# Perceiver, layer 0: a seven-operation weight decode, heads turned earlier, Newton last on GpSimd, and spare buffers in the opening

## The chip, the core and the metric

The kernel runs on one core of a Trainium2 chip, in float32 for nearly all of its matmuls. The metric is the device time of one launch in microseconds; the time of a version is the median of its runs. Five engines work side by side, each through its own list of instructions in order: TensorE (PE; its weight loads are PEld), VectorE (DVE), ScalarE (ACT), GpSimd (POOL) and SyncE (SP), which in this kernel issues nearly all DMAs.

## The reference

`x` is 64 sequences of 32 rows of 256 numbers, and `ctx` 64 sequences of 257 such rows. Six blocks follow one another, each on the layer norm of `x` and added to it:

```python
x = x + _L0_xattn_ref(_layernorm(x), ctx_1024, ctx_1024, ...)
x = x + _L0_attn_ref(_layernorm(x), ...)
x = x + _L0_ffn_ref(_layernorm(x), L0_ffn_weight, L0_ffn_weight_scale, L0_ffn_bias)
x = x + _L1_xattn_ref(_layernorm(x), ctx_1024, ctx_1024, mask, ...)
x = x + _L1_attn_ref(_layernorm(x), ...)
x = x + _L1_ffn_ref(_layernorm(x), ...)
```

The change lies in layer 0. Its two attentions have 16 heads of 16, are causal over 32 positions (the first attends to the first 32 rows of the context), and turn queries and keys by rotary angles: `x1 * cos - x2 * sin`, `x1 * sin + x2 * cos`. Its feed-forward block rounds its input and its weights to 8-bit floats with 4 exponent and 3 mantissa bits ("coarse" numbers). The weights come to the kernel as bytes:

```python
x_scale = jnp.maximum(amax, 1e-12) / FP8_MAX
qinput = (x / x_scale).astype(FP8)
A = qinput.astype(x.dtype) * x_scale
Bm = weight.astype(x.dtype) * weight_scale
out = jnp.einsum('bsk,nk->bsn', A, Bm) + bias
```

Layer 1 (a cross attention over all 257 rows, a gated mixer, a routed mixture of eight experts) is left as it is.

## The kernel before, in words

`x` stays on the chip in four tiles `xs[g]` of 512 rows, each as four row tiles of 128. Layer 0's two attentions on four such groups give eight groups, n = 0 to 7, and `small_attentions` runs them through one hand-written pipeline. All instructions are kept in the order of the program on each engine, so an instruction that waits holds up all behind it on its engine.

The opening loads the inputs (`first_loads`, a generator that issues a few DMAs at each `next`), normalises group 0 and rotates its keys and queries. After it each group n takes four steps, t = 0 to 3, and a step does a piece for several groups:

- `scores`, `sums`, `turned`, `context`, `by_feature` and `project` belong to the row tiles of groups already prepared. A tile goes through them over five steps (the list `line`): scores with `mx` and `sc` on DVE and `e` on ACT; then its sums; then e turned by PE (`ps_t`, `eT`) and the context `o`; then `by_feature` turns the heads' output on PE (`ps_c`) and ACT writes `cT`; then `project` multiplies `cT` by the output weights (`ps_p`) and DVE adds the result to `x`.
- `rotated` prepares the group n+1: one half of its keys (t = 0, 1) or queries (t = 2, 3). PE computes `ps_qk`, DVE writes `part` (times sine), four DMAs copy `part` into `far` with its 32-row blocks swapped, ACT and POOL make `near` (times cosine). It returns an add, `near + far` on POOL, which goes into the list `adds` and writes `kT` or `qT`.
- `spread_keys` writes `kb`, the blocks of keys, from `kT`: in each of a step's two parts one or two of them on ACT, and one on POOL in the first part.
- `values` (t = 0 and 2) computes `v` and writes it to DRAM; `blocks` (t = 3) reads it back into `vb` with eight DMAs.
- `norm_steps` normalises the group n+2, in pieces called through `prepare`: statistics in t = 0; their aggregate, the first guess `r0` and three Newton steps for the root in t = 1 (twelve operations on 128x4 on POOL; for n = 0 nine on DVE); the rows `y` of two tiles in t = 2 and of two in t = 3. `opened` then turns `y` into `yT`.
- `add_bias` adds the output bias row to `x` on POOL.
- `decode_fp8` makes the coarse weights `w8` from the bytes `raw`, two DVE operations a call, on one half of the weights at a time. `first_sides` works on the feed-forward block of the first row group from n = 6 on, and needs `w8` in n = 7.

The adds of a step run early in the next one if that is a t = 0, and late otherwise:

```python
due, adds = adds, []
if t == 0:
    for add in due:
        add()
    due = []
```

Buffers come in rings: `part` has two (p0, p1), `near` two (n0, n1), `far` three; the scores' bank on PE, `pair_bank`, is one. In the opening, keys and queries of group 0 share the rings.

Of the kernel before, what the change touches and what calls it, by code (L numbers as in the profile page):

```python
# [7 lines left out]
F32 = mybir.dt.float32  # L8
BF16 = mybir.dt.bfloat16
I32 = mybir.dt.int32  # L10
U8 = mybir.dt.uint8
AF = mybir.ActivationFunctionType
ALU = mybir.AluOpType
# [3 lines left out]
P = 128  # L17
D = 256
NB, S, SK = 64, 32, 257
H, DH = 16, 16  # L20
NG, NT = 4, 4
GT = NT * P
# [17 lines left out]
R_XO0, R_AO0, R_FF, R_XO1, R_GO, R_SB2, R_RB = 0, 256, 512, 768, 1024, 1280, 1536  # L40
# [24 lines left out]
def perceiver_kernel(ctx: ExitStack, tc: tile.TileContext, a: dict, out: bass.AP):  # L65
# [54 lines left out]
    def turn(ps, src, eye):  # L120
        return kept(nc.tensor.transpose(ps, src, eye))  # L121

    def norm_steps(g, eng=None, apart=False, ts=range(NT), by_act=False):

        x = xs[g]
        n, t0 = len(ts), ts[0]
        st = small.tile([P, n, 6], F32, tag="st", name="st")
        mv = small.tile([P, n, 2], F32, tag="mv", name="mv")
        for t in range(n):
            vector.bn_stats(st[:, t, :], x[:, t0 + t, :])  # L130
        if apart:
            yield
        for t in range(n):
            vector.bn_aggr(mv[:, t, :], st[:, t, :])

        ve = small.tile([P, n], F32, tag="ve", name="ve")
        vector.tensor_scalar(ve, mv[:, :, 1], EPS, None, ALU.add)
        half = small.tile([P, n], I32, tag="half", name="half")
        vector.tensor_scalar(half, ve.bitcast(I32), 1, None, ALU.logical_shift_right)
        r0 = small.tile([P, n], I32, tag="r0", name="r0")  # L140
        vector.tensor_scalar(r0, half, -1.0, float(0x5F3759DF), ALU.mult, ALU.add)
        r = r0.bitcast(F32)
        for _ in range(3):
            sq = small.tile([P, n], F32, tag="sq", name="sq", bufs=6)
            rn = small.tile([P, n], F32, tag="rn", name="rn", bufs=6)
            if eng is vector:
                vector.tensor_tensor(sq, r, r, ALU.mult)
                vector.scalar_tensor_tensor(sq, sq, -0.5, ve, ALU.mult, ALU.mult)
                vector.scalar_tensor_tensor(rn, sq, 1.5, r, ALU.add, ALU.mult)
            else:  # L150
                gpsimd.tensor_tensor(sq, r, r, ALU.mult)
                gpsimd.tensor_tensor(sq, sq, ve, ALU.mult)
                gpsimd.tensor_scalar(sq, sq, -0.5, 1.5, ALU.mult, ALU.add)
                gpsimd.tensor_tensor(rn, sq, r, ALU.mult)
            r = rn
        if by_act:
            off = small.tile([P, n], F32, tag="off", name="off")
            gpsimd.tensor_scalar(off, mv[:, :, 0], -1.0, 1.0, ALU.mult, ALU.mult)
            gpsimd.tensor_tensor(off, off, r, ALU.mult)
        yield  # L160
        y = ypool.tile([P, n, D], F32, tag="y", name="y")
        for t in range(n):
            if by_act:
                scalar.activation(
                    y[:, t, :],
                    x[:, t0 + t, :],
                    AF.Identity,
                    bias=off[:, t : t + 1],
                    scale=r[:, t : t + 1],
                )  # L170
            else:
                vector.tensor_scalar(
                    y[:, t, :],
                    x[:, t0 + t, :],
                    mv[:, t, 0:1],
                    r[:, t : t + 1],
                    ALU.subtract,
                    ALU.mult,
                )
            if t == 1 and n > 2:  # L180
                yield
        return y
# [46 lines left out]
    def proj(ps, w, rhs):  # L229

        for k in range(2):
            mm(ps, lhsT=w(k), rhs=rhs(k), start=(k == 0), stop=(k == 1))
# [13 lines left out]
    def small_attentions(layers, first_loads, decode, sides, load_layer1, layer1):  # L246
# [51 lines left out]
        def opened(it):  # L298
            yT = transposed(it["y"], pa, yTs([P, 2, GT], "yT"))
            it["yT"] = yT  # L300
            if not it["from_ctx"]:
                it["kvT"] = yT

        def rotated(it, i, c):

            src, cs, sn = (
                (it["kvT"], cos, sin) if i == 1 else (it["yT"], cosq, sinq)
# [5 lines left out]
            w, v0 = it["w"], it["v0"]  # L313
            ps = pa([P, GT], "ps_qk")
            proj(ps, lambda k: w[:, i, k, c * P : (c + 1) * P], lambda k: src[:, k, :])

            def by_place(table):
                return table.rearrange("p (o q) -> p o q", o=1).to_broadcast([P, 16, S])
# [2 lines left out]
                return tile_.rearrange("p (b q) -> p b q", q=S)  # L321

            bias = vec[:, v0 + 2 * i + c : v0 + 2 * i + c + 1]
            part = part_([P, GT], "part")
            vector.scalar_tensor_tensor(
                by_seq(part), by_seq(ps), bias, by_place(sn), ALU.add, ALU.mult
            )
# [2 lines left out]
            for at in range(0, P, S):  # L330
                queue = scalar if (it["n"], i, c) == (0, 0, 1) and at >= 2 * S else sync
                queue.dma_start(out=far[at : at + S, :], in_=part[at ^ S : (at ^ S) + S, :])
            near = near_([P, GT], "near")
            if it["n"] > 0:
                scalar.activation(near, ps, AF.Identity, bias=bias)
                gpsimd.tensor_tensor(by_seq(near), by_seq(near), by_place(cs), ALU.mult)
# [166 lines left out]
        it = group(0, fetch(0))  # L503
        next(loads)
        after = group(1, fetch(1))
        next(loads)
        for half in range(2):
            clear(vbs[0][half], vector)
            clear(vbs[1][half], gpsimd)
# [13 lines left out]
            spread_keys(it, 0, 0, part)  # L523
        adds.append(rotated(it, 0, 0))
        adds.append(rotated(it, 0, 1))
        adds[1]()
        for part in range(2):
            spread_keys(it, 0, 1, part)
# [13 lines left out]
        for n in range(len(order) + 1):  # L542
# [3 lines left out]
                after["kb"] = [None, None]  # L546
            kvT = coming = None
            if n + 2 <= last:
                side = norm_steps(order[n + 2][1], None if n else vector, apart=True)
            else:  # L550
                side = sides

# [7 lines left out]
            for t in range(NT):  # L560
# [3 lines left out]
                if n <= last:  # L564
                    if t < 2:
                        kb_now = (now, 1, t)
                    elif after is not None:
                        kb_now = (after, 0, t - 2)
                due, adds = adds, []
                if t == 0:  # L570
                    for add in due:
                        add()
                    due = []
                if kb_now:
                    spread_keys(*kb_now, 0)
                if line[4]:
# [1 line left out]
                if after is None:  # L578
                    next(layer1, None)
                else:  # L580
                    y = prepare(t % 2 == 1)
                    adds.append(rotated(after, *((1, 0), (1, 1), (0, 0), (0, 1))[t]))
                if line[3]:
                    by_feature(line[3])
                prepare(t % 2 == 0)
                if n + 2 > last:
# [1 line left out]
                    next(side, None)  # L588
                if n > 0:
                    add_bias(n - 1, t)  # L590
                if n > 0 and (t % 2 == 0 or n + 2 > last):
                    next(decode, None)
                for add in due:
                    add()
                if kb_now:
                    spread_keys(*kb_now, 1)
                if after is None:
                    next(layer1, None)
                elif t % 2 == 0:
                    values(after, t // 2)  # L600
                    if (n, t) == (0, 0):
                        opened(after)
                elif t == 3:
                    for half in range(2):
                        blocks(after, half)
                    if n + 2 <= last:
                        coming = group(n + 2, kvT)
                        coming["y"] = y
                        opened(coming)
# [22 lines left out]
    def first_loads():  # L632
        def row_load(at, n=D):
            sync.dma_start(
                out=rows[:, at : at + n], in_=a["rows"][at : at + n].partition_broadcast(P)
            )
# [8 lines left out]
        sync.dma_start(out=xs[1], in_=x_view[1])  # L645
        yield
        sync.dma_start(out=xs[2], in_=x_view[2])
        sync.dma_start(out=w_cur[:, 3], in_=a["w_l0x"][:, 3])
        row_load(R_XO0)
        sync.dma_start(out=xs[3], in_=x_view[3])  # L650
        yield
        sync.dma_start(out=raw, in_=a["w_fp8"])
        for at in (R_AO0, R_FF, R_XO1, R_GO):
            yield
            row_load(at)
        for i in range(0, 4, 2):
# [9 lines left out]

    def decode_fp8():

        scratch = sb.tile([P, 4, D], F32, tag="yT", name="scratch")
        u, neg, e_f, scale = (scratch[:, i, :] for i in range(4))  # L670
        bits = scale.bitcast(I32)
        for c in range(2):
            vector.tensor_copy(u, raw[:, c * D : (c + 1) * D])
            vector.tensor_scalar(neg, u, 128.0, None, ALU.is_ge)
            yield
            vector.scalar_tensor_tensor(u, neg, -128.0, u, ALU.mult, ALU.add)
            vector.tensor_copy(bits, u)
            yield
            vector.tensor_scalar(bits, bits, 3, None, ALU.logical_shift_right)
            vector.tensor_copy(e_f, bits)  # L680
            yield
            vector.scalar_tensor_tensor(u, e_f, -8.0, u, ALU.mult, ALU.add)

            vector.tensor_scalar(bits, e_f, 1.0, 120.0, ALU.max, ALU.add)
            yield
            vector.tensor_scalar(bits, bits, 23, None, ALU.logical_shift_left)

            vector.tensor_scalar(e_f, e_f, 1.0, None, ALU.min)
            yield
            vector.scalar_tensor_tensor(u, u, 0.125, e_f, ALU.mult, ALU.add)  # L690
            vector.tensor_tensor(u, u, scale, ALU.mult)
            yield
            vector.tensor_scalar(neg, neg, -2.0, 1.0, ALU.mult, ALU.add)
            vector.tensor_tensor(w8[:, c, :], u, neg, ALU.mult)
            yield

    def linear(g):

# [1355 lines left out]
```

## The time and the profile before

| | |
|---|---|
| time, median of 3 runs | 929.61 us (929.5 to 930.77) |
| profiled execution, its own time | 928.56 us |
| its span, first to last instruction | 926.8 us |
| mean granted clock of PE over the span | 0.973 |
| busy share: PE, PEld, DVE, ACT, POOL | 92%, 63%, 65%, 46%, 54% |
| DVE's first operation on scores (`mx`) | 31.41 us |
| DVE's last `sc` of layer 0 | 223.37 us |
| 40 to 225 us, busy: PE, DVE, ACT, POOL | 170.7, 159.2, 112.8, 125.6 us |

In a row of the timeline the first number is the start in us from the beginning of the span, the second the duration from the first to the last of the instructions that the row joins (x2, x4); then come engine, line, operation, output<-inputs and shapes. SPq and ACTq rows are issues of DMAs. Brackets give how long the engine had been idle ahead of the row and what ended that; where a wait is for several things, the one named is the one that came last by the profile. L106 and L118 are lines of helpers that issue all operations, so rows are told apart by their tiles. A row `q1 ...` or `far<-part SPq ...` of the page's last part gives size and median time from issue to landing.

### The profile page before, as it was taken

What the parts mean: (1) busy time and instruction counts of PE and PEld (TensorE: products, weight loads), DVE (VectorE), ACT (ScalarE), POOL (GpSimd) and SP (SyncE); (2) the same over time, 40 slices, a digit from 0 to 9 for tenths busy, and PEclk for the clock granted to TensorE, in tenths of its full rate; (3) what the DMA queues carried; (4) which work ended last, traced back from release to release, by engine and by line L of the source; (5) the groups of instructions that cost most, each with busy time, mean ns of one, the idle gap of its engine ahead of it and who ended that gap; (6) DMA issues with size and microseconds to landing.
All of it is one profiled execution on the core that took longest, in us unless ns stands there. A gap on an engine that the chain in (4) does not pass through costs nothing. (4 is left out here: it accounts for less than half of the span.)

```text
span 926.8 us, 22828 instructions
## 1 busy us (share of the span) xinstructions
PE 856.0 (92%) x8699; PEld 588.5 (63%) x8699; DVE 605.3 (65%) x1755; ACT 424.1 (46%) x1099; POOL 501.1 (54%) x982
## 2 busy tenths in 40 slices
PE   6899999979899999999999999999889889999993
PEld 3566666656456666666656666565656648888882
DVE  7888888897677677675777666878654872111116
ACT  2566666645555555554555456564443212222210
POOL 3567667764674656564664747656531214555430
PEclk9999999989999999999999999999799979999997
DMA  7445333543110111111110112000001046777758
GB/s 240 140 133 141 85 88 101 132 115 104 53 52 8 46 53 53 52 54 52 53 52 3 52 52 98 2 2 24 2 23 35 24 143 189 235 240 229 216 182 272
DMA packets 66926, 88.79 MB, mean 96 GB/s; under 512 B 32480, under 2 KB 50688, under 8 KB 64768
## 3 DMA queue, kind: packets, MB, share of 16 engines
q1 hardware_dynamic: 63264, 77.75, 27.6%
q0 software_dynamic: 3456, 9.44, 3.1%
q8 instruction: 69, 1.13, 0.5%
q14 instruction: 41, 0.34, 0.1%
q10 hardware_dynamic: 96, 0.13, 0.1%
HBM read 65.80 MB, written 13.11 MB: 85 GB/s over the span
## 5 line engine op out<-in xcount | busy, mean ns | idle before, releaser
L106 ACT ACTIVATE e<-e,xnm 128x257 f32<-128x257 f32 x256 | 127.2, 498 | 51.5 <-DVE xnm L106 45.5
L106 DVE CUSTOM_DVE_ANT_0 e<-ps_s,mask 128x257 f32<-128x257 f32 x256 | 93.5, 421 | 49.6 <-PE ps_s L118 47.9
L118 PE MATMUL ps_k<-ct,w_w_l1x 128*128 128x512 f32 x256 | 122.3, 600 | 1.6 <-ACT yT L106 0.6
L106 POOL TENSOR_SCALAR e<-e,xsm 128x256 f32<-128x256 f32 x256 | 121.8, 496 | 0.0
L118 PE MATMUL ps_v<-w_w_l1x,ct 128*128 128x256 f32 x512 | 121.8, 381 | 0.0
L121 PE MATMUL ps_t<-cst,e 128*128 128x128 f32 x640 | 102.9, 284 | 7.8 <-DVE eT L106 6.9
L106 DVE COPY eT<-ps_t 128x512 f32<-128x512 f32 x128 | 88.0, 687 | 30.3 <-PE ps_t L121 30.1
L118 PEld LDWEIGHTS ps_v<-w_w_l1x,ct 128*128 128x128 f32 x512 | 93.9, 191 | 11.0 <-issue 0.2
L106 POOL TENSOR_TENSOR x<-x,rows 128x256 f32<-128x256 f32 x96 | 71.3, 759 | 46.2 <-ACT y L106 19.4
L106 ACT ACTIVATE kT<-ps_k,vec 128x512 f32<-128x512 f32 x64 | 44.1, 689 | 100.5 <-PE ps_k L118 100.3
L121 PEld LDWEIGHTS ps_t<-cst,e 128*128 128x128 f32 x640 | 72.1, 142 | 26.4 <-DVE eT L106 7.8
L106 ACT ACTIVATE hTr<-ps_h,w 128x256 f32<-128x256 f32 (+1 forms) x80 | 31.4, 450 | 115.0 <-issue 82.7
L106 DVE TENSOR_TENSOR og<-ps_o,b 128x512 f32<-128x512 f32 (+1 forms) x20 | 12.8, 638 | 105.6 <-PE ps_o L118 105.6
L118 PEld LDWEIGHTS ps_k<-ct,w_w_l1x 128*128 128x128 f32 x256 | 44.5, 190 | 41.3 <-issue 35.3
L1817 POOL DMA_INDIRECT r_rows<-og,lv x36 | 35.6, 989 | 60.9 <-DVE og L106 56.0
L118 PE MATMUL ps_h<-ygT,w 128*128 128x256 f32 (+1 forms) x320 | 65.8, 359 | 0.6 <-issue 0.6
L118 PE MATMUL ps_o<-w,hTr 128*128 128x256 f32 x288 | 65.3, 379 | 0.0
L106 ACT COPY v<-ps_v 128x512 f32<-128x512 f32 x80 | 46.4, 582 | 39.5 <-PE ps_v L118 39.4
L106 POOL TENSOR_TENSOR last<-e,xsm 128x4 f32<-128x4 f32 x64 | 13.0, 204 | 88.4 <-DVE xsm L106 88.0
L118 PEld LDWEIGHTS ps_h<-ygT,w 128*128 128x128 f32 x320 | 54.9, 190 | 6.6 <-issue 0.8
L118 PEld LDWEIGHTS ps_o<-w,hTr 128*128 128x128 f32 x288 | 54.4, 190 | 7.2
L106 ACT ACTIVATE kb<-kT,cst 128x256 f32<-128x256 f32 x96 | 45.4, 512 | 26.7 <-POOL kT L106 25.1
(210 smaller groups left out, 1677.2 us busy)
## 6 DMA issues: line engine op xcount, KB each, us to landing
ct<-in_ctxT SPq DMA_DIRECT2D x16, 1024.0 KB, 5.4
w<-in_ew SPq DMA_DIRECT2D x20, 514.0 KB, 3.6
w<-in_ew SPq DMA_DIRECT2D x20, 512.0 KB, 3.7
far<-part SPq DMA_DIRECT2D x126, 64.0 KB, 2.3
v_rows<-v SPq DMA_DIRECT2D x16, 256.0 KB, 2.3
vb<-v_rows SPq DMA_DIRECT2D x64, 64.0 KB, 2.1
r<-r_rows SPq DMA_DIRECT2D x8, 512.0 KB, 8.2
b<-in_eb SPq DMA_DIRECT2D x20, 128.0 KB, 3.8
```

The source lines that it names most:

```text
L106: ins = getattr(self.engine, name)(*args, **kw)
L118: return kept(nc.tensor.matmul(ps, **args))
L121: return kept(nc.tensor.transpose(ps, src, eye))
L1817: wrote = nc.gpsimd.indirect_dma_start(out=r_rows, out_offset=bass.IndirectOffsetOnAxis(ap=write_i[:, at : at + 1], axis=0), in_=o[:, i, : ...
```

## The change

- `decode_fp8`: the byte is shifted so that its exponent and mantissa stand in a float's places, 120 is added to the exponent, small numbers are mended by `u + min(u - 2^-6, 0)`, and the sign is put on. Seven operations on all 512 columns replace 13 on 256 for each half, one a call instead of two, and it is called in even steps alone.
- The adds of a step all run at the head of the next step.
- `rotated` takes the tile whose heads are due and calls `by_feature` right behind its own matmuls, so `ps_c` and `cT` come ahead of `part` and `near` in the order.
- `norm_steps` has one more pause, between `r0` and Newton; Newton is called late in t = 1, behind the key blocks' second part.
- In the opening the keys of group 0 get `part` and `near` in buffers that the scores use later (sc0, sc1, e0, e1). The third set of loads is issued behind the first queries, and the loads are cut into other sets, so that the output weights, the first bias row and `x` of groups 2 and 3 come later, and the bytes `raw` at the end of step t = 3 of n = 0 instead of t = 1.
- `opened` of group 1 moves from step t = 0 of n = 0 to t = 1.

```diff
-    def norm_steps(g, eng=None, apart=False, ts=range(NT), by_act=False):
+    def norm_steps(g, eng=None, apart=False, ts=range(NT), by_act=False, split=False):
...
         r = r0.bitcast(F32)
+        if split:
+            yield
         for _ in range(3):
...
-        def rotated(it, i, c):
+        def rotated(it, i, c, between=None):
...
             proj(ps, lambda k: w[:, i, k, c * P : (c + 1) * P], lambda k: src[:, k, :])
+            if between:
+                by_feature(between)
+            spare = (it["n"], i) == (0, 1)
...
-            part = part_([P, GT], "part")
+            part = sb.tile([P, GT], F32, tag=f"sc{c}", name="part") if spare else part_([P, GT], "part")
...
-            near = near_([P, GT], "near")
+            near = sb.tile([P, GT], F32, tag=f"e{c}", name="near") if spare else near_([P, GT], "near")
...
         after = group(1, fetch(1))
-        next(loads)
...
         adds.append(rotated(it, 0, 1))
+        next(loads)
         adds[1]()
...
-                side = norm_steps(order[n + 2][1], None if n else vector, apart=True)
+                side = norm_steps(order[n + 2][1], None if n else vector, apart=True, split=True)
...
-                due, adds = adds, []
-                if t == 0:
-                    for add in due:
-                        add()
-                    due = []
+                for add in adds:
+                    add()
+                adds = []
...
-                    adds.append(rotated(after, *((1, 0), (1, 1), (0, 0), (0, 1))[t]))
-                if line[3]:
+                    adds.append(rotated(after, *((1, 0), (1, 1), (0, 0), (0, 1))[t], line[3]))
+                if line[3] and after is None:
                     by_feature(line[3])
...
-                if n > 0 and (t % 2 == 0 or n + 2 > last):
+                if n > 0 and t % 2 == 0:
                     next(decode, None)
-                for add in due:
-                    add()
                 if kb_now:
                     spread_keys(*kb_now, 1)
+                prepare(t == 1)
                 if after is None:
                     next(layer1, None)
                 elif t % 2 == 0:
                     values(after, t // 2)
-                    if (n, t) == (0, 0):
-                        opened(after)
+                elif (n, t) == (0, 1):
+                    opened(after)
...
         sync.dma_start(out=xs[2], in_=x_view[2])
+        yield
         sync.dma_start(out=w_cur[:, 3], in_=a["w_l0x"][:, 3])
         row_load(R_XO0)
+        yield
         sync.dma_start(out=xs[3], in_=x_view[3])
         yield
         sync.dma_start(out=raw, in_=a["w_fp8"])
-        for at in (R_AO0, R_FF, R_XO1, R_GO):
+        row_load(R_AO0)
+        for at in (R_FF, R_XO1, R_GO):
             yield
             row_load(at)
...
-        scratch = sb.tile([P, 4, D], F32, tag="yT", name="scratch")
...
+        scratch = sb.tile([P, 2, 2 * D], F32, tag="yT", name="scratch")
+        u, v = (scratch[:, i, :] for i in range(2))
+        bits = u.bitcast(I32)
+        vector.tensor_copy(bits, raw)
+        yield
+        vector.tensor_scalar(
+            bits, bits, 127, 20, ALU.bitwise_and, ALU.logical_shift_left
+        )
+        yield
+        vector.tensor_scalar(bits, bits, float(120 << 23), None, ALU.add)
+        yield
+        vector.tensor_scalar(v, u, -(2.0**-6), 0.0, ALU.add, ALU.min)
+        yield
+        vector.tensor_tensor(u, u, v, ALU.add)
+        yield
+        vector.tensor_scalar(v, raw, 128.0, -2.0, ALU.is_ge, ALU.mult)
+        yield
+        vector.scalar_tensor_tensor(
+            w8.rearrange("p c d -> p (c d)"), v, 1.0, u, ALU.add, ALU.mult
+        )
+        yield
```

More of the change, by code (lines that the diff above doesn't have):

```diff
@@ L667, in decode_fp8 @@
     def decode_fp8():
-        scratch = sb.tile([P, 4, D], F32, tag="yT", name="scratch")
[L670 to L695, printed above, removed]
+        scratch = sb.tile([P, 2, 2 * D], F32, tag="yT", name="scratch")
[19 more added lines that the diff above has]
+        yield
     def linear(g):
```

## The prediction, on record before the result

> **What bounds the kernel now.** I read the page's busy shares first: PE 92%, DVE 65%. The chain that ended last begins at 761 us and says nothing about layer 0, so for the stretch the change touches I went to the timeline, engine by engine, and then to the table of stages.
>
> A group of layer 0 takes four steps, t = 0 to 3; I call that a round and mark its end by T, the start of `part` in step t = 3. From the `part` rows T is 43.78, 67.91, 92.40, 117.26, 142.22 and 167.18 for groups 0 to 5, then 194.55. First the timeline's rows of one round (start, duration, instruction; in brackets the idle time ahead and who ended it):
>
> ```profile
> 93.22 2.74 SPq L106 DMA_DIRECT2D far<-part  x4
> 96.06 4.01 SPq L106 DMA_DIRECT2D vb<-v_rows  x8
> 100.18 3.05 SPq L106 DMA_DIRECT2D far<-part  x4
> 98.28 0.76 DVE L106 SCALAR_TENSOR_TENSOR part<-ps_qk,vec,cst 128x512 f32<-128x512 f32 x1 [1.12 <-PE ps_qk L118]
> 100.26 1.84 DVE L106 TENSOR_SCALAR scratch<-scratch 128x256 int32<-128x256 int32 x2
> 105.90 0.20 POOL L106 TENSOR_TENSOR sq<-r 128x4 f32<-128x4 f32 x1 [3.45 <-DVE r L106]
> 107.97 1.13 PE L118 MATMUL ps_p<-w_w_l0x,cT 128*128 128x256 f32 x4 [1.26 <-ACT cT L106]
> 109.15 1.27 POOL L106 TENSOR_TENSOR near<-near,cst 128x512 f32<-128x512 f32 x1
> 110.37 0.73 POOL L106 TENSOR_TENSOR x<-x,rows 128x256 f32<-128x256 f32 x1
> 111.05 1.27 POOL L106 TENSOR_TENSOR kT<-near,far 128x512 f32<-128x512 f32 x1
> 111.53 1.28 DVE L106 TENSOR_SCALAR y<-x,mv,rn 128x256 f32<-128x256 f32 x2
> 113.72 0.68 DVE L106 TENSOR_REDUCE mx<-pair_bank 128x16 f32<-128x512 f32 x1
> 117.26 0.74 DVE L106 SCALAR_TENSOR_TENSOR part<-ps_qk,vec,cst 128x512 f32<-128x512 f32 x1
> ```
>
> PE pauses about 1.7 us a round (1.26 here for cT, 0.5 for yT in t = 0), so of 24.9 us some 23.2 are PE's own. DVE is full from one `part` to the next except for some 3.5 us of short waits. The ceiling on steady rounds is therefore 1.7 us each, whatever is taken off DVE. SP matters too: eight vb issues stand between the far copies of t = 3 and those of t = 0.
>
> Next, the opening, the place where the weight bytes arrive, and the end of the layer:
>
> ```profile
> 18.08 0.75 DVE L106 SCALAR_TENSOR_TENSOR part<-ps_qk,vec,cst 128x512 f32<-128x512 f32 x1 [2.25 <-DMA far<-part]
> 31.41 0.69 DVE L106 TENSOR_REDUCE mx<-pair_bank 128x16 f32<-128x512 f32 x1 [1.13 <-PE pair_bank L118]
> 47.05 5.10 SPq L106 DMA_DIRECT2D vb<-v_rows  x8
> 52.19 0.45 SPq L106 DMA_DIRECT2D rows<-in_rows  x1
> 50.92 1.10 DVE L106 CAST scratch<-raw 128x256 f32<-128x256 uint8 x1
> 199.55 1.36 DVE L106 TENSOR_TENSOR w<-scratch 128x256 bf16<-128x256 f32 x1
> 202.63 0.69 PE L121 MATMUL ps_c<-cst,o 128*128 128x128 f32 x2 [3.50 <-DVE o L106]
> far<-part SPq DMA_DIRECT2D x126, 64.0 KB, 2.3
> ```
>
> DVE has no wait of any size from 173.06 to about 210, and PE idles for it (1.37, 0.92, 1.14, 3.50 us): here DVE is the bound.
>
> **The decode.** The 26 old operations on 128x256 take 19.4 us in all (timeline rows of scratch): 0.29 us where nothing disturbs, 1.1 where a GpSimd operation is under way. Seven on 128x512 replace them, one in each even step, finished by group 4. The nearest rows of that width are 0.55 (int32 tensor_scalar, at 195.21) to 0.69 (tensor_tensor); I take 0.75 with disturbance, between 0.4 and 1.6. In groups 1 to 5 the saving falls on DVE time in front of PE-bound waits. In groups 6 and 7 it is on the path: from the first decode row of a step to its mx it is 0.55 + 1.47 + 1.20 + 2.13 = 5.35 us. **Tail: -5.4** (between -2, if PE's order takes over, and -7, PE's idle there).
>
> TensorE is granted 0.50 in 204 to 208, after that 3.5 us gap. [...]
>
> **The opening.** The keys' part and near get buffers of their own, so the 2.25 us wait at 18.08 goes, and 1.4 MB (x2, x3, one weight matrix, one row) leave the queue ahead of the far copies. What is late next: kT's add waits for its far copies (18.03 now, perhaps 16.5), then the queries' far copies (four issues of 0.65 us a piece on SP), q's adds at about 24.7 instead of 26.0; the transposes of group 1 no longer stand ahead of the first scores. DVE then has its normalisation and bn_stats of x2, which is now issued on SP behind 14 far copies, near 22, and lands some 4 to 6 us later (x: 6.2 median in the first 60 us). I put the first mx at 27.9 instead of 31.41. From mx to T0 DVE is full (12.4 us) and keeps that length. **Opening: -3.5** (0 to -5).
>
> **The steady round.** cT ahead of near takes cT off the wait for `part`; it ends PE's 1.26 us wait if nothing else is late. But the adds now stand at the head of each step, and GpSimd executes in order. In t = 1 the kT add needs the far copies of t = 0, which SP issues only after the eight vb. Counted from T: far 0.8 to 3.6, vb to 7.7, far again to 10.8, the last issue at 10.1; landing 2.3 later (the page's median): 12.4. Then GpSimd does add 1.27, the keys' block 0.55, near 1.22, row bias 0.7 and, last, Newton: 3.3 from 105.90 to 109.2. Sum 7.0 with gaps: r is ready at T + 19.4. `y` in t = 2 needs r; now y starts at T + 19.1, because Newton came ahead of near, bias and add. Then y 1.28, decode 0.75 and 3.54 from mx to the next `part` (113.72 to 117.26). So T' = T + 25.0 with a decode operation and 24.2 without, against 24.9 now. PE's wait for cT turns into DVE's wait for Newton. Behind y wait mx, sc, o and `part` on DVE; PE waits for o.
>
> Round by round, with the issue times of its own rows: group 2 has a slower vb (5.46) and a row load behind it, far lands at 13.4: 25.9 against 24.49, +1.4. Group 3 has one row load in front: 25.3 against 24.86, +0.5. Group 4 decodes nothing in t = 2: 24.2 against 24.96, -0.8. Group 5 (far rows end later, 13.4): 25.2 against 24.96, +0.2.
>
> Group 1 is worse, because the byte load moves from t = 1 to t = 3 of group 0, where it is issued behind the vb copies: T0 + 8.4, landed 10.75 with the 2.3 us of other 64 KB transfers. The first decode operation, which DVE reaches at T0 + 7.1 (50.92 less 43.78), waits 3.6 us, and mx, o and `part` of t = 1 wait behind it. `part` at 15.3, near on ACT to 16.9, near on GpSimd, bias, Newton to 22.15, then 1.28 + 0.75 + 3.54: 27.7 against 24.13, +3.6. **Rounds: +4.9.** Bounds: -4 if far lands so early that PE sets every round, +8 if y also waits out the next add.
>
> [...] Row: y's first operation took 0.95 and its second 0.33 while the kT add had 0.79 us to run, so y waited for the end of an add; I keep 1.28 for the pair. [...]
>
> **Sum.** -3.5 + 4.9 - 5.4 = -4.0 us, of the profiled execution's 928.56 (span 926.8): 924.56. The median of three runs is 929.61, 1.05 above it, so I forecast 925.6.
>
> **Rivals.** (1) *Far lands in time and PE sets the rounds*: each of groups 2 to 5 saves 1.5 us, group 1 loses 2: -3.5 - 4 - 5.4, 916.7. For it: cT's wait is plain in every round. Against: SP's issue rows are full from T to T + 10.8. Chance 0.12. (2) *Slower: GpSimd's add in t = 1*, held by SP's order, delays Newton and with it y by more than I count. It decides once far lands later than T + 14 or y waits out the add; then rounds cost +9, the opening gives only 2 because x2 comes late, and the tail 4: 932.6. For it: vb took 5.1 to 5.5 us in groups 0 and 1, and loads move behind it. Against: 4.0 later. Chance 0.25. (3) *No change*: gains and losses cancel, the decode's cycles being free where PE or SP sets the pace; 929.6. Chance 0.20.
>
> My forecast, faster by 2 to 7 us, gets 0.43. A measurement of this kernel can tell about 0.2% (1.86 us) from no change. Faster: 0.43 + 0.12 = 0.55, same 0.20, slower 0.25. Range 918 to 932, which leaves out most of rival 1 and the end of rival 2; the forecast's own is 922.5 to 927.7.
>
> **What would show it.** Right: first mx near 28; T0 near 40; a DVE wait of 3 to 4 us for raw at T0 + 7; GpSimd idle ahead of kT's add in t = 1 until some 12.4 us after T, and a DVE wait for rn ahead of y in t = 2; PE without its 1.26 us wait for cT; rounds of 25 us; DVE in groups 6 and 7 some 5 us shorter. Wrong: rounds near 23.3 (no such chain), no wait for raw (the byte load landed sooner), or PE idle past 200 as long as before.

## The result and the profile after

The changed kernel takes 939.42 us, median of 6 runs (934.88 to 943.35), against 929.77 for the kernel before on the same chip: a ratio of 1.0099, 95% interval 1.0077 to 1.0121. The forecast was 925.6 us with a range of 918 to 932; it is slower by 9.7 us instead. The profiled execution is the longest of the six, 943.35 us with a span of 941.6 us. The six spans run from 933.1 us at a mean granted clock of 0.973 to 941.6 us at 0.963: on the whole the longer runs have the lower clock. All that is read from the trace below belongs to this longest execution; it lies 14.8 us above the profiled execution of before (928.56 us), where the medians differ by 9.7.

From the page of the kernel after, the busy shares (engine, busy us, share of the span, instructions): they are within a point of those of before, and tell nothing of the loss.

```profile
PE 864.7 (92%) x8699; PEld 595.1 (63%) x8699; DVE 602.4 (64%) x1734; ACT 425.9 (45%) x1099; POOL 497.6 (53%) x982
```

The timeline of the kernel after, round of group 3 (T = 100.15 to 128.69), rows of SP, DVE, POOL and PE; these stand against the first rows of the prediction:

```profile
103.48 4.00 SPq L106 DMA_DIRECT2D vb<-v_rows  x8
108.08 2.42 SPq L106 DMA_DIRECT2D far<-part  x4
106.75 0.75 DVE L106 SCALAR_TENSOR_TENSOR part<-ps_qk,vec,cst 128x512 f32<-128x512 f32 x1 [1.29 <-PE ps_qk L118]
107.53 0.45 SPq L106 DMA_DIRECT2D rows<-in_rows  x1
108.73 1.49 DVE L106 TENSOR_TENSOR scratch<-scratch 128x512 f32<-128x512 f32 x1
113.19 1.28 POOL L106 TENSOR_TENSOR kT<-near,far 128x512 f32<-128x512 f32 x1 [2.38 <-DMA far<-part]
113.36 1.14 DVE L106 TENSOR_SCALAR ve<-mv 128x4 f32<-128x4 f32 x1
115.19 0.75 DVE L106 SCALAR_TENSOR_TENSOR part<-ps_qk,vec,cst 128x512 f32<-128x512 f32 x1
116.82 1.28 POOL L106 TENSOR_TENSOR near<-near,cst 128x512 f32<-128x512 f32 x1 [1.90 <-ACT near L106]
118.74 0.22 POOL L106 TENSOR_TENSOR sq<-r 128x4 f32<-128x4 f32 x1
121.84 0.20 POOL L106 TENSOR_TENSOR rn<-sq,rn 128x4 f32<-128x4 f32 x1
122.02 1.26 POOL L106 TENSOR_TENSOR kT<-near,far 128x512 f32<-128x512 f32 x1
122.07 1.85 DVE L106 TENSOR_SCALAR y<-x,mv,rn 128x256 f32<-128x256 f32 x2 [2.67 <-POOL rn L106]
123.84 1.48 DVE L106 TENSOR_SCALAR scratch<-raw 128x512 f32<-128x512 uint8 x1
127.03 0.44 PE L121 MATMUL ps_c<-cst,o 128*128 128x128 f32 x2 [2.78 <-DVE o L106]
128.69 0.75 DVE L106 SCALAR_TENSOR_TENSOR part<-ps_qk,vec,cst 128x512 f32<-128x512 f32 x1
```

The chain is the forecast one: SP's vb issues, then far, GpSimd idle 2.38 us ahead of kT's add, near, Newton (twelve operations, 118.74 to 122.04), then y, on which DVE waited 2.67 us, and behind it o, for which PE waited 2.78 us. In the kernel before, the last rn stands at 109.2, T + 16.8; here at T + 21.9. Far lands later, near waits, and y and the decode operation take longer than forecast; only the way from mx to the next `part`, 3.45 us for 3.54, does not. A round of 28.54 us has come of one of 24.86. Far was held here by SP's list and by a late `part` nearly alike: the `part` of t = 0 ends at 107.50, and SP is done with vb and the row load behind it at 107.98. No run moved the vb issues, so SP's share is read from these rows and not tested.

The waits of the kernel after from 40 to 235 us (us in total, times, longest):

```profile
POOL kT L106 <- DMA far<-part: 18.2, 5, 5.4
PE ps_c L121 <- DVE o L106: 16.2, 8, 3.9
DVE y L106 <- POOL rn L106: 13.9, 5, 3.6
DVE scratch L106 <- DMA raw<-in_w_fp: 4.1, 1, 4.1
```

The same waits of the kernel before; no row there has y waiting for rn:

```profile
PE ps_p L118 <- ACT cT L106: 8.0, 7, 1.4
PE ps_c L121 <- DVE o L106: 5.8, 3, 3.5
```

The wait for cT is gone and a larger one has come.

The table of stages of the kernel after, cut at the steps of the granted clock to within 0.05 us (stretch, length, then busy us and instructions of PE, PEld, DVE, ACT, POOL; PEclk; DMA share; GB/s):

```profile
96.89:100.30 3.41, 1.11 (x8) 0.79 (x8) 3.34 (x9) 2.03 (x5) 2.15 (x3) 0.99 0.38 111
100.30:103.71 3.41, 3.41 (x78) 2.49 (x78) 1.75 (x3) 2.44 (x5) 1.95 (x2) 0.51 0.22 56
...
124.19:127.60 3.41, 0.63 (x6) 0.57 (x6) 3.34 (x5) 0.92 (x2) 3.39 (x4) 0.99 0.00 0
127.60:131.01 3.41, 2.92 (x55) 1.72 (x57) 1.83 (x5) 2.59 (x8) 0.71 (x1) 0.50 0.09 23
```

The two stretches in which PE works for 1.11 and 0.63 of 3.41 us are followed by one and by two at half clock: the half clock stands right behind PE's pause for o. Up to 239 us the kernel after has 30.7 us at half clock in six places, three of 3.41 us and three of 6.8 (from 127.6, 182.3 and 216.4 us); before has 10.2 us (from 30.8 and 201.5).

The opening, the arrival of the bytes and the end of the layer, timeline of the kernel after:

```profile
16.55 0.75 DVE L106 SCALAR_TENSOR_TENSOR part<-ps_qk,vec,cst 128x512 f32<-128x512 f32 x1 [0.31 <-PE ps_qk L118]
28.91 0.67 DVE L106 TENSOR_REDUCE mx<-pair_bank 128x16 f32<-128x512 f32 x1
34.60 3.02 PE L118 MATMUL ps_qk<-yT,w_w_l0x 128*128 128x512 f32 x4 [2.88 <-ACT yT L106]
47.18 5.89 SPq L106 DMA_DIRECT2D vb<-v_rows  x8
55.30 0.43 DVE L106 CAST scratch<-raw 128x512 int32<-128x512 uint8 x1 [4.09 <-DMA raw<-in_w_fp]
197.78 3.54 DVE L106 TENSOR_SCALAR y<-x,mv,rn 128x256 f32<-128x256 f32 x4
203.03 0.44 PE L121 MATMUL ps_c<-cst,o 128*128 128x128 f32 x2 [1.30 <-DVE o L106]
217.47 0.69 PE L121 MATMUL ps_c<-cst,o 128*128 128x128 f32 x2 [3.92 <-DVE o L106]
```

The part of 18.08 has lost its 2.25 us and the first mx comes 2.50 us sooner, but T0 is 43.91 (before 43.78), because PE stands 2.88 us for group 1's yT. The bytes cost 4.09 us, for 3.6 forecast. At the end of the layer neither PE's waits nor the half clock have gone: the last sc is at 238.21, 14.84 us later than before.

Split at the T's, those 14.84 us are: opening +0.13 (forecast -3.5), group 1 +5.59 (29.72 against 24.13; forecast +3.6), groups 2 to 5 +9.91 (109.18 against 99.27; forecast +1.3), tail after T5 -0.79 (55.40 against 56.19; forecast -5.4).

### The profile page after: what moved, and what is told of

The parts are those of the page before. It is cut to its first block, busy times and chain, and to the rows that moved or that the text cites. A ratio compares the mean times of both kernels' runs of the same rounds, so it can differ in the third digit from the quotient of the medians.

```text
span 941.6 us, 22800 instructions
## 1 busy us (share of the span) xinstructions
PE 864.7 (92%) x8699; PEld 595.1 (63%) x8699; DVE 602.4 (64%) x1734; ACT 425.9 (45%) x1099; POOL 497.6 (53%) x982
## 3 DMA queue, kind: packets, MB, share of 16 engines
q1 hardware_dynamic: 63264, 77.75, 27.2%
## 5 line engine op out<-in xcount | busy, mean ns | idle before, releaser
L106 POOL DMA_INDIRECT yg<-y_rows,lv x36 | 35.1, 975 | 39.8 <-DVE lv L106 29.1
```

What stands on the lines that cost most here:

```text
L106: ins = getattr(self.engine, name)(*args, **kw)
```

## The experiments

The theory at the start: y in t = 2 waits for Newton, which GpSimd reaches last, behind an add held by SP's far copies. The rivals: the adds at the head do the harm by themselves; the late bytes do; the decode or cT ahead costs something that is not seen. Times are medians; "ratio" is against the kernel before on the same chip, where it took 929.77 us (after), 929.84 (e1 to e4), 929.23 (e5 to e8), 931.22 (e9 to e12) and 929.48 (e13 to e15), so that between chips the ratios are the better measure. The other columns come from one profiled execution each: "2 to 5" is T5 - T1, the rounds of groups 2 to 5; "half" is the time at half clock up to 260 us. T0 itself moves by about 1 us between executions: e5, whose edit acts only behind it, has 44.79 for 43.78.

| kernel | us | ratio, 95% interval | T0 | group 1 | 2 to 5 | last sc - T5 | half |
|---|---|---|---|---|---|---|---|
| before | 929.77 | | 43.78 | 24.1 | 99.3 | 56.2 | 10.2 |
| after | 939.42 | 1.0099 (1.0077-1.0121) | 43.91 | 29.7 | 109.2 | 55.4 | 30.7 |
| e1 Newton back | 932.09 | 1.0020 (1.0004-1.0037) | 46.51 | 27.0 | 101.9 | 52.4 | 17.1 |
| e2 adds back | 941.46 | 1.0142 (1.0103-1.0181) | 44.16 | 29.4 | 107.9 | 53.5 | 20.5 |
| e3 both back | 926.71 | 0.9960 (0.9946-0.9975) | 45.59 | 26.7 | 95.7 | 52.7 | 13.7 |
| e4 bytes early | 937.96 | 1.0091 (1.0061-1.0120) | 43.86 | 26.7 | 108.1 | 53.2 | 20.5 |
| e5 decode only | 923.00 | 0.9919 (0.9894-0.9945) | 44.79 | 23.5 | 96.7 | 52.7 | 10.2 |
| e6 cT ahead only | 927.69 | 0.9981 (0.9968-0.9994) | 44.71 | 24.2 | 98.7 | 55.3 | 10.2 |
| e7 decode, cT | 921.59 | 0.9908 (0.9880-0.9937) | 44.73 | 23.5 | 95.7 | 52.1 | 3.4 |
| e8 and spare buffers | 919.69 | 0.9897 (0.9871-0.9924) | 42.94 | 23.7 | 95.7 | 52.1 | 3.4 |
| e9 Newton on DVE | 940.15 | 1.0100 (1.0085-1.0116) | 43.32 | 28.4 | 109.9 | 51.4 | 27.3 |
| e10 work added to PE | 936.46 | 1.0065 (1.0041-1.0090) | 43.49 | 29.0 | 104.6 | 52.6 | 13.7 |
| e11 e3, opened back | 923.90 | 0.9927 (0.9913-0.9941) | 42.60 | 26.7 | 95.7 | 52.2 | 3.4 |
| e12 e9, opened, bytes | 938.88 | 1.0083 (1.0064-1.0101) | 45.55 | 26.7 | 109.2 | 53.0 | 27.3 |
| e13 one Newton step | 921.63 | 0.9912 (0.9882-0.9941) | 43.78 | 27.2 | 94.9 | 51.0 | 3.4 |
| e14 y late | 930.23 | 1.0015 (0.9995-1.0035) | 44.59 | 26.9 | 101.5 | 51.8 | 13.7 |
| e15 e14, opened, bytes | 930.66 | 1.0011 (0.9993-1.0028) | 43.88 | 25.8 | 102.9 | 53.9 | 13.7 |

Outside the range that was expected came out e2 (slower), e5 (faster), e9 and e12 (slower), e13 (faster) and e15 (slower), and by less than 0.5 us e10 and e14.

**e1 to e4: the kernel after with parts undone.**

e1, Newton ahead of near again:

```diff
-side = norm_steps(..., apart=True, split=True)
+side = norm_steps(..., apart=True)
...
-                prepare(t == 1)
```

> The changed kernel with Newton called again ahead of near in t = 1; the adds stay at the head of each step, the byte load stays late. Theory (GpSimd's order delays r, and y and DVE wait for it): r is ready some 2 to 3 us sooner after the kT add, DVE's wait for rn ahead of y falls from 13.9 us in five rounds to under 4, rounds of groups 2 to 5 come down from 26-28 us to 25-26, time 930 to 934 us. Rival (the late bytes alone): nothing gained but noise, 937 to 941 us.

e2, the adds that run in t = 1 to 3 late again, Newton last; e3 makes both edits:

```diff
-                for add in adds:
-                    add()
-                adds = []
+                due, adds = adds, []
+                if t == 0:
+                    for add in due:
+                        add()
+                    due = []
...
+                for add in due:
+                    add()
                 if kb_now:
                     spread_keys(*kb_now, 1)
```

> The changed kernel with the adds of t = 0, 1, 2 again late in the next step; Newton stays last on GpSimd. Theory: the kT add no longer holds the key block and near in t = 1, but Newton still stands behind near, bias and add: little is won, rounds 25.5 to 27 us, 933 to 938 us. If the head position of the adds alone were the cause, the rounds would go back to 24.5 and the time under 929 us. Rival (late bytes): 937 to 941 us.

> The changed kernel with both the adds and Newton in the old places. What is left of the change: the seven-operation decode, cT ahead of near, the opening and the late bytes. Theory: no wait of DVE for rn is left, rounds 2 to 5 at 23.5 to 24.5 us; group 1 keeps its wait for the bytes (4 us): 923 to 928 us. Rival (late bytes alone are the loss): about 937 us still.

e4, the bytes in t = 1 of group 0, where they were before:

```diff
         row_load(R_XO0)
+        sync.dma_start(out=raw, in_=a["w_fp8"])
         yield
...
-        sync.dma_start(out=raw, in_=a["w_fp8"])
         row_load(R_AO0)
```

> The changed kernel with the bytes loaded in t = 1 of group 0 as before, together with the output weights; all else as changed. Theory (GpSimd's order): the 4.1 us wait for raw is gone but group 1's Newton is then held by the kT add, so only 1 to 3 us come back: 936 to 939 us. Rival (late bytes): the loss of 10 us goes, 927 to 931 us.

The two orders don't add up. Against e3, Newton last costs 12.2 us in groups 2 to 5 (e2), the adds at the head 6.2 (e1), both 13.5 (after). Undoing the adds alone gives no gain (e2; 933 to 938 us were expected), undoing Newton alone 7.3 us, both 12.7. In e2 Newton still stands behind near, bias and the add, and rn is ready at T + 21.6 in group 3's round, as in after (21.9); in e1 at T + 18.6, but there near starts at T + 18.5 instead of e3's T + 15.9, since Newton's 3.3 us stand in front of it. With the adds at the head GpSimd's list in t = 1 begins at T + 13 only, and it is too long whichever of near and Newton comes last. Early bytes shorten group 1 by 3.0 us, and group 2's round, 28.7 instead of 26.5, takes most of that back; the 1.5 us of e4 are within its interval.

**e5 to e8: the kernel before with parts added.** e5 has `decode_fp8` of the change, called in even steps; e6 has `between` in `rotated` (cT ahead of near); e7 both; e8 also the keys' spare buffers, with the loads in their old order:

```diff
+        bits = u.bitcast(I32)
+        vector.tensor_copy(bits, raw)
...
-                if n > 0 and (t % 2 == 0 or n + 2 > last):
+                if n > 0 and t % 2 == 0:
...
+            if between:
+                by_feature(between)
...
+            spare = (it["n"], i) == (0, 1)
+            part = sb.tile([P, GT], F32, tag=f"sc{c}", name="part") if spare else part_([P, GT], "part")
...
```

> The kernel before with the seven-operation decode alone (called in even steps). Theory (DVE's time in groups 1 to 5 lies beside PE's wait for cT; in groups 6 and 7 it is on the path): rounds of groups 2 to 5 shorten by no more than 0.5 us each, groups 6 and 7 by 3 to 5 us in all: 924.5 to 927 us. Rival (decode is free everywhere): 929 to 930 us. Rival (DVE bounds every round): over 10 us gained, under 920.

> The kernel before with by_feature called inside rotated, so that ps_c and cT come ahead of part and near, and nothing else. Theory: PE's wait for cT (1.3 us in each of five rounds) goes and little takes its place while DVE still carries the old decode: rounds 24.2 to 24.6 us instead of 24.9, 925 to 928 us. Rival (cT's wait only hides another wait): 929 to 930 us.

> Both of these on the kernel before: the decode and cT ahead of near; adds, Newton, loads and opening as before. Theory: rounds of groups 1 to 5 at 23.7 to 24.2 us, as in the run with adds and Newton put back, but without its losses in the opening (T0 1.8 us late) and at the bytes (2.6 us): 919 to 923 us. Rival (the gain of that run came from the opening): 926 to 929 us.

> The same with the spare buffers for the keys' part and near of group 0, loads in the old order. Theory: the 2.25 us wait of DVE at 18 us goes, the first mx comes 1 to 2.5 us earlier, and as nothing behind it is moved, T0 follows by 0.5 to 2 us: 917 to 922 us, 0.5 to 2 us below the run without. Rival (SP's order of far and vb copies sets T0): no difference to it.

All three parts pay: the decode 6.2 us (2.6 of them in groups 2 to 5 and 3.5 behind T5 by the traces), cT ahead 1.5, both 7.6, and the spare buffers bring 1.9 more (that last step, between two kernels of four runs each, is smaller than their intervals; T0 in the traces moves by 1.8, and by 1.05 counted from the first `part`). e8 is the fastest kernel of the study, faster than both kernels, by 9.5 us than before. So the loss lies in what it leaves out: the adds' and Newton's order, opened, and the loads.

**e9 and e12: Newton off GpSimd.** `norm_steps` gets `vector` for every group; e12 also puts opened and the bytes back.

```diff
-side = norm_steps(order[n + 2][1], None if n else vector, ...)
+side = norm_steps(order[n + 2][1], vector, ...)
```

> After, but Newton runs on DVE for all groups (nine operations of 0.16 to 0.2 us, the form that group 0 already uses), at the same late place in t = 1; the adds stay at the head of a step, the bytes stay late. Theory A (y is late because Newton stands last on GpSimd, behind an add that is held by SP's far copies): DVE's wait for rn ahead of y goes altogether, although GpSimd still waits as long for far; DVE takes 1.7 us more a round; rounds of groups 2 to 5 fall from 26.2 to 28.5 us to 24.5 to 25.5; 929 to 933 us. Rival B (the adds at the head are themselves what delays near, kb and the scores): another wait takes the place of rn's, PE still pauses 2 to 3 us a round, 936 us or more.

> After with Newton on DVE, opened of group 1 back in t = 0 and the bytes loaded in t = 1 of group 0: of the change's order only the adds at the head of a step and cT ahead of near are left, with the decode and the spare buffers. Theory A: no long wait for rn or raw is left, T0 near 43, rounds near 24.5 to 25, 920 to 925 us: the adds' place alone costs nothing or a little against e8 (919.69). Rival B: the adds at the head cost 1 us or more a round even with Newton elsewhere, 927 us or more.

The wait for rn went, but the expected gain didn't come: 940.15 and 938.88 us. This seemed to speak against the first theory. Timeline of e12, DVE and POOL in t = 1 of group 3's round:

```profile
112.86 0.70 DVE L106 TENSOR_TENSOR sq<-r 128x4 f32<-128x4 f32 x1
113.60 0.41 DVE L106 SCALAR_TENSOR_TENSOR sq<-sq,ve 128x4 f32<-128x4 f32 x1
114.04 1.21 DVE L106 SCALAR_TENSOR_TENSOR rn<-sq,r 128x4 f32<-128x4 f32 x1
115.29 0.65 DVE L106 TENSOR_TENSOR sq<-rn 128x4 f32<-128x4 f32 x1
113.97 1.26 POOL L106 TENSOR_TENSOR near<-near,cst 128x512 f32<-128x512 f32 x1
```

DVE's operations on 4 columns took 0.16 us here where GpSimd was idle (the last five of this chain, 115.97 to 116.92), but the one that began 0.07 us after near took 1.21 us. The nine took 4.1 us here, not the 1.7 they had been priced at, in front of mx, o and `part`; PE waited 2.8 us for o all the same. One load had taken the place of another, so these two runs can't tell whether GpSimd's order or the adds' place sets the rounds.

**e10: more work for PE.** Six turns of the identity go into ps_c ahead of its own two, for the tile whose heads are turned in t = 2; they compute nothing.

```diff
             ps_c = po([P, 2, P], "ps_c")
+            if tile_s["t"] == 3 and tile_s["now"]["n"] < 6:
+                for c in range(6):
+                    turn(ps_c[:, c % 2, :], ident, ident)
```

> After, with work added that computes nothing: six turns of the identity (0.22 us each, 1.3 us in all) into ps_c ahead of its own two turns in step t = 2 of groups 1 to 6, where PE would stand still for o. Theory C (PE's pauses of 1.9 to 2.8 us bring the halved clock behind them, and the halved clock lengthens the rounds): the halved stretches at 59.4, 100.3 and 127.6 us go or shrink, rounds of 28 us fall by 1 to 2 us, 931 to 936 us. Rival D (the halved clock falls where PE has slack, and Newton's order alone sets the rounds): the halved stretches may go, but the rounds stay and the time is 938 to 942 us.

Timeline of e10, PE:

```profile
115.44 0.82 PE L121 MATMUL ps_c<-cst 128*128 128x128 f32 x6
...
124.02 0.44 PE L121 MATMUL ps_c<-cst,o 128*128 128x128 f32 x2 [1.36 <-DVE o L106]
```

They take 0.82 us and land one step ahead of the pause, not in it as the expectation had it: the pause is in t = 3. They still fill time, as DVE sets when o comes: the pause is 1.36 us instead of 2.78, the time at half clock falls from 30.7 to 13.7 us, and groups 2 to 5 take 104.6 us instead of 109.2. The median is 3.0 us below that of after, the ratio 0.0034 lower, with intervals that overlap a little. More work on PE gave a time that is lower if anything. If the filler acts through the clock alone, some 3 us of the 10 are the clock's; the traced rounds give 4.6, but the traced execution of after is the longest of its six.

**e11: opened of group 1 back in t = 0**, on e3:

```diff
                     values(after, t // 2)
-                elif (n, t) == (0, 1):
-                    opened(after)
+                    if (n, t) == (0, 0):
+                        opened(after)
```

> As e3 (adds and Newton at their old places), and opened of group 1 back in step t = 0 of group 0; the bytes stay late. If the move of opened is what cost the opening its gain: PE's idle time of 4.65 us for yT near 36 us goes, T0 falls from 45.59 to about 43, 923 to 925 us; the wait for raw in group 1 stays. If yT is late for another reason: T0 stays near 45.6, 926 to 927 us.

923.90 us, T0 42.60 instead of 45.59. The row of e3's timeline that went away:

```profile
36.34 3.62 PE L118 MATMUL ps_qk<-yT,w_w_l0x 128*128 128x512 f32 x4 [4.65 <-ACT yT L106]
```

So the move of opened takes 3.0 us at T0 (2.5 counted from the first `part`), more than the 1.9 us that the spare buffers bring in e8.

e11 differs from e8 in the loads alone, e3 from e11 in opened, after from e3 in the order of adds and Newton. By the ratios the 19 us between the fastest kernel and the changed one come in these three steps: the loads some 3 us (intervals overlap; group 1 takes 26.7 us for 23.7, the wait for the bytes), opened 3, and GpSimd's order 13.

**e13 to e15: the dose and the consumer.** e13 takes one Newton step in place of three in the groups that GpSimd serves, so that two refinements of the norm's root are left out and it is coarser; e14 leaves Newton alone and computes all four of y in t = 3; e15 is e14 with opened and the bytes back.

```diff
-        for _ in range(3):
+        for _ in range(1 if split and eng is None else 3):
```
```diff
+                    prepare(t == 3)
                     y = prepare(t % 2 == 1)
...
-                prepare(t % 2 == 0)
+                prepare(t == 0)
```

> After, with one Newton step in place of three on GpSimd for groups 3 to 7 (four operations of 128x4 in place of twelve, some 2.2 us less ahead of y; the norm's root is then coarser, which leaves out part of the computation). Theory A (y in t = 2 waits for Newton at the end of GpSimd's list, and all of DVE and PE behind it): the five waits of DVE for rn, 13.9 us in all, shrink to under 4 us, rounds of groups 2 to 5 fall by 1.5 to 2.2 us each from 109.2 us in all to 101 to 103, 930 to 934 us. Rival E (y's wait is beside the path; something else, such as near behind the add, sets the rounds): the wait shrinks and another grows, 937 to 941 us.

> After, with y of the first two row tiles computed in t = 3 beside that of the last two, so that what needs Newton comes 6 us later; Newton, the adds, opened and the bytes stay as in after. Theory A: no wait for rn is left, PE's 2 to 3 us pauses in t = 2 and the halved clock behind them go, rounds of groups 2 to 5 near 24 to 25 us (98 us in all against 109.2), 926 to 930 us. Rival B (the adds at the head delay near, kb and the scores by themselves): rounds stay at 26 us or more (104 us in all), 934 us or more.

> As e14, and opened of group 1 back in t = 0, the bytes loaded in t = 1 of group 0: the decode, cT ahead, the spare buffers, the adds at the head and Newton last are all in, but nothing waits for Newton early. Theory A: T0 near 42.5, no wait for raw, 919 to 923 us, as e8 (919.69) or e11 (923.9). Rival B: 927 us or more.

Timeline of e13, POOL and DVE, group 3's round (T = 94.50):

```profile
106.82 1.28 POOL L106 TENSOR_TENSOR kT<-near,far 128x512 f32<-128x512 f32 x1 [2.92 <-DMA far<-part]
111.58 0.21 POOL L106 TENSOR_TENSOR sq<-r 128x4 f32<-128x4 f32 x1
112.44 0.20 POOL L106 TENSOR_TENSOR rn<-sq,r 128x4 f32<-128x4 f32 x1
112.68 1.71 DVE L106 TENSOR_SCALAR y<-x,mv,rn 128x256 f32<-128x256 f32 x2 [0.43 <-POOL rn L106]
118.70 0.73 DVE L106 SCALAR_TENSOR_TENSOR part<-ps_qk,vec,cst 128x512 f32<-128x512 f32 x1
```

Eight operations fewer, 2.2 us in each of five rounds, 11 us of GpSimd's work, give some 17.5 us, each kernel taken against before on its chip: 921.63. The adds are still at the head, GpSimd still waits 2.92 us for far, opened and the bytes are still late. rn is ready at T + 18.1 instead of 21.9, the five waits of y for it shrink from 13.9 to 2.5 us, groups 2 to 5 take 94.9 us, and the rounds have no half clock left. So with the adds at the head the rounds are as short as e3's (95.7) once GpSimd gets through its list by about T + 18: this answers what e9 left open. It does not make the adds' place free with a full list behind it, which is e1's 6.2 us. That e13 gives more than was expected (930 to 934) fits the cause of the loss: 3.75 us less to rn are 2.24 of Newton itself, 0.72 because the kT add begins at T + 12.3 instead of 13.0 (the `part` of t = 0 comes at T + 5.35 instead of 6.60, with no half clock ahead of it), and 0.79 less between that add and Newton.

e14 takes the consumer away and gets back some 9 us, no more; its rounds take 101.5 us where 98 were expected. Timeline of e14, DVE and PE at the end of group 2's round:

```profile
93.21 3.73 DVE L106 TENSOR_SCALAR y<-x,mv,rn 128x256 f32<-128x256 f32 x4
96.60 0.95 PE L121 MATMUL psT<-cst,y 128*128 128x128 f32 x4 [0.82 <-DVE y L106]
```

Four of y in a row take 3.73 us beside GpSimd's add and near, straight ahead of `part`, and PE waits for y in their place. e15 took 930.66 us, so it missed the 919 to 923 expected: what opened and the bytes give back in e11 does not show behind that wait.

## Why the prediction was wrong

**The mechanism was found, its place in the sum was not.** Far landed at T + 13.0 in group 3's round (forecast 12.4), the wait for cT went, y waited for rn, the bytes cost 4.1 us (forecast 3.6). This is rival 2, the slower one, which I gave 0.25 and 932.6 us; the rounds cost 15.5 us, not the 9 of that rival or the 4.9 of the forecast. Of its two conditions one came true in every round, y beside an add; the kT add began later than T + 14 in group 1 alone (14.2; 13.0 to 13.8 in groups 2 to 5). The forecast was -4.0 us and the two traced executions lie 14.8 apart: of these 18.8 us the rounds are 10.6, the tail 4.6 and the opening 3.6.

**Newton's due time: T + 19.4 was T + 21.9.** The step that failed is "GpSimd does add 1.27, the keys' block 0.55, near 1.22, row bias 0.7 and, last, Newton" as one list without waits. near needs ACT, ACT needs `ps_qk` and its own order, and DVE, which had to do the decode operation and ve first, spent 1.49 and 1.14 us on them beside GpSimd's near and add (rows above). The decode operation takes 1.48 to 1.50 us in all fifteen traces that have it; ve took 0.17 us in e13 with GpSimd idle (106.45). GpSimd stood 1.90 us ahead of near. Counting GpSimd's own work alone left out that it waits for engines whose operations last longer beside it.

**y and the decode beside the adds.** I kept 1.28 us for the pair of y's and 0.75 for a decode operation. They took 1.85 and 1.48 us: y begins 0.05 us after the kT add and lasts past its end, the decode operation begins 0.10 us after near. With GpSimd idle a pair of y's took 0.72 us in after (128.05). In each of the five rounds of after in which y waits for rn, the first y of the pair began within 0.1 us of the start of the kT add and took 1.36 or 1.37 us; one with GpSimd idle took 0.40. The row behind the 1.28 had caught only the last 0.79 us of an add. The forecast's bound of +8, for a y that waits out the add, has no run behind it; measured in group 3's round are 1.85 us for the pair, 0.57 above the 1.28. The forecast of a round with a decode operation, 25.0 us, becomes the measured 28.5 with 2.5 us for the late rn, 1.1 for y and decode, and 0.1 less behind them. In e8 pairs of y take 1.8 to 2.2 us as well and the rounds stay at 24.2 or less; on the path they come by the late rn.

**The clock was no term of mine.** I looked at one pause of 3.5 us and did not ask what the new pauses of 2 to 3 us would do. After has 30.7 us at half clock, e13 3.4, and the rows fit a loop: a late rn, a pause of PE, half clock, a late `part`, a late far, a later rn. e10 alone tests it, and its intervals overlap. In the seventeen traces, from 15 to 260 us, each of the 40 steps of 3.41 us at full clock with PE busy for up to 1.46 us was followed by half clock, 13 of 59 with 1.47 to 2.10 us, and 1 of 1045 with more; in before and after alone 5 of 5, 3 of 7 and none of 117. The two stretches ahead of the half clock in the table of stages were not idle, with PE busy 1.11 and 0.63 us in them.

**The opening: -3.5 was +0.1.** mx came at 28.91 for 27.9. "From mx to T0 DVE is full (12.4 us) and keeps that length" failed: it took 15.0 us. Where opened stands in t = 0 and the adds in their old places it does keep it (12.4 in e5 to e8 and in e11), and in e3, where only opened is moved of these, it is 16.7. I had listed the move of opened from t = 0 to t = 1 and priced it nowhere. With the adds at the head, putting opened back did not settle it (15.0 us in e9 and also in e12, which has it back; 15.6 in e14 and 13.4 in e15, which has it back), so its share in after itself is not shown.

**The tail: -5.4 was -0.8.** The direction was right as to the decode: from T5 to the last sc e5 gains 3.5 us, e7 4.1, e13 5.2. The seven operations took 9.06 us in after, six of them 1.2 to 1.5 us each, and 7.3 in e5, against 5.25 at the forecast's 0.75; the old ones are 28, fourteen for each half and not thirteen, and took 19.5 us. In after the trace shows against the term two stretches of 6.8 us at half clock (from 182.3 and 216.4 us; before has one) and the four of y taking 3.54 us beside GpSimd; how much each takes back wasn't tried. I had sized each term with the others at rest.

What stays open: how the 9.9 us of groups 2 to 5 divide exactly between wait and clock (e10 shrinks both), what SP's order of issues adds, and why e14 with e15's two edits gains nothing.

## What to carry to other kernels

Ask of an operation that is moved to the end of an engine's list when its result is due, and add to the list what that engine waits for, above all engines whose operations last longer beside its own (here ve on DVE, 1.14 us for 0.17); the short operations at the end of this list cost more than their own length (11 us of work, some 17.5 us of time), with PE pausing behind them. Price a change's parts alone and together, and every move in the diff: here three parts gave 9.5 us together, and the moves beside them took 19. Count PE's pauses together with the half clock behind them: here, with pauses of 2 to 3 us, 30.7 us of it up to 239 us, against 10.2 before.

## What the runs showed of the hardware

- In before and after, up to 260 us, half clock came in four stretches of 3.41 us and four of 6.83, and PE was not idle for the whole of the step ahead of any. In the seventeen traces PE busy for up to 1.46 us of 3.41 was followed by it every time (40 of 40), 1.47 to 2.10 us sometimes (13 of 59), more than that once in 1045. In after 1.73 us (from 55.88) was followed by it and 1.92 us (from 69.54) was not.
- Added PE work that computes nothing (0.82 us a round) went with a lower time, 936.46 against 939.42 us (1.0065 and 1.0099 of before, intervals overlapping).
- In e12 operations of DVE on 4 columns took 0.16 us with GpSimd idle, and 1.21 us when GpSimd had begun one on 128x512 0.07 us earlier. The same decode operation, on the same bytes, took 0.41 us in e13, begun 0.09 us after GpSimd's `kb` on 128x256, and 1.48 in after, begun 0.10 us after near on 128x512.
